# Radix-2 halves for the two transforms over the height

## The chip, the cores and the metric

One core of one Trainium2 chip. The metric is the device time of one launch in microseconds (us). Names of lines (L303) are those of the kernel in question, so the same operation has another line after the change.

## The reference, cut to what matters

Four images of 256 x 256 positions with 64 channels pass through a block with a 2-D FFT and an inverse FFT, then a depthwise convolution, then a second layer. Cut to what the change touches:

```
h  = pw(layernorm(x), w_te)              # x: (4, 256, 256, 64)
F  = fft2(h, axes=(1, 2))                # height and width
fc = gelu(pw(concat(real F, imag F), w_fc))
sp = real(ifft2(re + 1j * im))
x1 = x + pw(sp, w_tp)
d  = gelu(depthwise3x3(pw(layernorm(x1), w_fe)))
out = second_layer(x1 + pw(d, w_fp))     # untouched here
```

The kernel does every transform as matmuls with tables of cosines and sines. The rows of an image lie on 128 partitions in two planes, t = 0 (rows 0 to 127) and t = 1 (rows 128 to 255).

## The kernel before

For each image there is a **forward stage** (layernorm and transform over the height), a **middle stage** (transform over the width, mixing of channels, width transform back) and a **convolution stage** (inverse transform over the height, layernorm, convolution). The forward stage takes 16 columns at a time, which is called a chunk here:

```
def layernorm(pool, src, dst, sq, name):
    nc.vector.tensor_reduce(mean, fl(src), AX.X, ALU.add)              # "mean"
    nc.vector.tensor_scalar(mean, mean, -1.0 / C, None, ALU.mult)      # small op: releases POOL
    nc.gpsimd.tensor_tensor(fl(dst), fl(src), mean..., ALU.add)        # "subtraction"
    nc.scalar.activation(fl(sq), fl(dst), AF.Square)
    nc.vector.tensor_reduce(var, fl(sq), AX.X, ALU.add)                # "variance"
    nc.vector.tensor_scalar(var, var, 1.0 / C, EPS, ALU.mult, ALU.add) # small op: releases POOL
    nc.gpsimd.tensor_tensor(rstd, var, minus_half..., ALU.pow)         # "power"
    nc.vector.tensor_tensor(fl(dst), fl(dst), rstd..., ALU.mult)       # "multiply"
# [...]
for q in range(NCH):                     # 16 chunks; xt has 3 buffers, sq 1, the others 2
    # [...] load xt
    layernorm(pool, rows, rows, sq, n)
    for par, op in enumerate((ALU.add, ALU.subtract)):                 # "first adds"
        nc.vector.tensor_tensor(xb[:, :, par], xt[:, :, 0], xt[:, :, 1], op)
    for par in range(2):
        for m in range(2):
            ps = bank(...)
            for t in range(2):           # the whole height: two matmuls that accumulate
                nc.tensor.matmul(ps, dh[:, t, m * P : (m + 1) * P], xb[:, t, par]...,
                                 start=t == 0, stop=t == 1)
            nc.scalar.copy(yt[:, par, :, m, :], ps...)
    # [...] store yt
```

The order in which each engine gets its instructions is fixed when the kernel is built: the scheduler of the framework interleaves several chunks. The inverse transform, also 16 columns at a time:

```
for w0 in range(0, W, 8):
    for t in range(2):
        ps = bank(...)
        for r, tb in enumerate((ihr, ihi)):      # real and imaginary part, 128 frequencies each
            nc.tensor.matmul(ps, tb[:, t * P : (t + 1) * P], uc[:, w0 : w0 + 8, r, :],
                             start=r == 0, stop=r == 1)
        nc.vector.tensor_tensor(dst, dst, ps, ALU.add)
layernorm(pool, x1, xn, sq, n)
```

## Time and profile before

7713.2 us (median of three, 7713.06 to 7714.08). From the trace, the length of the stages of the second to fourth image, as means. (PE is TensorE, DVE VectorE, ACT ScalarE, POOL GpSimd.) A forward stage is counted from the last matmul of the image before to the first one of the middle stage, a convolution stage from its first matmul to its last:

| stage | us an image | bound by |
|---|---|---|
| forward | 317.6 | a loop of waits between DVE and POOL, 17.3 us a chunk |
| middle (to the first matmul of the next stage) | 579.1 | PE |
| convolution | 827.4 | PE, 50.13 us a period of 16 columns |

In a timeline a row is: start us, length us, engine, line, operation, out<-in, shape, count, and in brackets how long the engine had been idle and what ended that. Two rows whose records overlap by 0.1 us are pipelined. Work per chunk is best read as the difference between starts.

### The profile page before, as it was taken

The numbers are of one execution on the slowest core, as the hardware profiler recorded it, in microseconds if no ns is written. First come the engines' busy times: TensorE is split into PE (matmuls) and PEld (weight loads), VectorE is DVE, ScalarE is ACT, GpSimd is POOL, SyncE is SP. The second block draws the span as 40 slices with busy tenths as digits, with TensorE's granted clock in tenths as the row PEclk, the third lists the DMA queues.
The fourth block names the chain that finished last, engine by engine and source line by source line (L and its number), as shares of the span: only waits on it lengthen the run. The fifth ranks groups of instructions, "written<-read, shape, count | busy, mean of one in ns | idle before, by whom it ended". The sixth has DMA issues, their size and how long they took to land.

```text
span 7717.2 us, 68181 instructions
## 1 busy us (share of the span) xinstructions
PE 6763.2 (88%) x28276; PEld 3952.8 (51%) x28276; DVE 2489.1 (32%) x2808; ACT 1726.7 (22%) x2514; POOL 1864.8 (24%) x718
## 2 busy tenths in 40 slices
PE   4699899994799899984799899975799899988888
PEld 1366555551466455541466455542466455544444
DVE  6433222316433322226333322226333232211111
ACT  2233211112233211112233211112233211111111
POOL 5311222215311222215311222215211222210000
PEclk8899999997899999997899999987899999999999
DMA  3222211223222222123222122213222222225555
GB/s 125 90 55 66 71 55 58 58 45 124 82 66 55 77 61 60 57 48 115 81 60 65 67 66 66 60 39 120 77 56 65 71 61 65 60 62 183 178 182 163
DMA packets 763659, 620.34 MB, mean 80 GB/s; under 512 B 279173, under 2 KB 689239, under 8 KB 754903
## 3 DMA queue, kind: packets, MB, share of 16 engines
q1 hardware_dynamic: 763350, 615.99, 26.5%
q8 instruction: 224, 3.67, 0.2%
q14 instruction: 85, 0.69, 0.0%
HBM read 347.49 MB, written 268.44 MB: 80 GB/s over the span
## 4 chain that ended last, share of the span: by engine, by line
PE 81%; DVE 7%; POOL 5%; issue 3%; DMA 3%; ACT 1%; SPq 0%; POOLq 0%; ACTq 0%; DVEq 0%
PE ps_h L565 17%; PE ps_p L380 12%; PE ps_h L575 9%; PE ps_x L360 6%; PE ps_f L611 6%; PE ps_o L702 6%; PE ps_s_c L509 6%; PE ps_u L443 6%; PE ps_z L426 6%; POOL rstd L273 4%; DVE xt L274 2%; PE ps_h L597 2%; DVE xb L298 2%; PE ps_m L687 2%; PE ps_t L533 2%
## 5 line engine op out<-in xcount | busy, mean ns | idle before, releaser
L565 PE MATMUL ps_h<-tt,wc_main 128*128 128x512 f32 x3072 | 1371.1, 596 | 0.0
L303 PE MATMUL ps_y<-xb,tab 128*128 128x512 f32 x1024 | 565.4, 713 | 642.8 <-DVE xb L298 642.8
L390 ACT ACTIVATE g<-ps_p,b_fc 128x512 f32<-128x512 f32 (+1 forms) x1040 | 709.6, 684 | 1145.0 <-PE ps_p L380 1041.3
L565 PEld LDWEIGHTS ps_h<-tt,wc_main 128*128 128x128 f32 x3072 | 566.2, 189 | 643.4 <-issue 642.5
L575 PE MATMUL ps_h<-tt,wc_half 64*128 64x512 f32 (+1 forms) x3792 | 736.5, 520 | 0.0
L269 POOL TENSOR_TENSOR xn_c<-x_c,mean_c 128x2048 f32<-128x2048 f32 x64 | 231.5, 3617 | 2075.4 <-DVE mean_c L268 1977.1
L303 PEld LDWEIGHTS ps_y<-xb,tab 128*128 128x128 f32 x1024 | 229.4, 232 | 975.9 <-issue 894.5
L396 POOL TENSOR_TENSOR d<-g,g 128x512 f32<-128x512 f32 x260 | 326.7, 1257 | 1665.7 <-ACT g L390 1665.7
L599 ACT ACTIVATE h<-ps_h,b_conv 128x512 f32<-128x512 f32 x512 | 323.0, 681 | 1751.1 <-PE ps_h L597 1751.1
L624 DVE TENSOR_TENSOR st<-x_c,ps_f 128x256 f32<-128x256 f32 x512 | 283.0, 594 | 1291.3 <-PE ps_f L611 1291.3
L575 PEld LDWEIGHTS ps_h<-tt,wc_half 64*128 64x128 f32 x3792 | 414.4, 185 | 349.2 <-issue 319.5
L426 PEld LDWEIGHTS ps_z<-w_tp,d 128*128 128x128 f32 x4064 | 493.7, 192 | 120.3 <-issue 103.3
L380 PE MATMUL ps_p<-xs,wp 128*128 128x512 f32 (+1 forms) x1040 | 528.8, 590 | 0.0
L380 PE MATMUL ps_p<-xs,wm 128*128 128x512 f32 (+1 forms) x1040 | 528.3, 589 | 0.0
L360 PE MATMUL ps_x<-tab,yb 128*128 128x128 f32 x4064 | 510.1, 279 | 0.0
L611 PE MATMUL ps_f<-w_fp,h 128*128 128x64 f32 x4096 | 505.5, 277 | 0.0
L509 PE MATMUL ps_s_c<-uc_c,tab 128*128 128x512 f32 x1024 | 462.7, 606 | 45.3 <-DMA uc_c<-u_d 45.3
L702 PE MATMUL ps_o<-xc,mt 128*128 128x512 f32 x1024 | 456.6, 599 | 50.0 <-DVE mt L695 50.0
L360 PEld LDWEIGHTS ps_x<-tab,yb 128*128 128x128 f32 x4064 | 483.3, 193 | 28.7 <-issue 28.7
L426 PE MATMUL ps_z<-w_tp,d 128*128 128x64 f32 x4064 | 481.7, 272 | 0.9 <-POOL d L396 0.9
L611 PEld LDWEIGHTS ps_f<-w_fp,h 128*128 128x128 f32 x4096 | 477.6, 192 | 0.0
L443 PE MATMUL ps_u<-zt,tab 128*128 128x512 f32 x1024 | 453.5, 596 | 3.5 <-DVE zt L429 3.5
(101 smaller groups left out, 6210.2 us busy)
## 6 DMA issues: line engine op xcount, KB each, us to landing
xt<-in_x_dram SPq DMA_DIRECT2D x128, 512.0 KB, 4.4
y_d<-yt SPq DMA_DIRECT2D x128, 512.0 KB, 2.6
yb<-y_d SPq DMA_DIRECT2D x128, 512.0 KB, 6.6
u_d<-ut SPq DMA_DIRECT2D x128, 512.0 KB, 3.3
uc_c<-u_d SPq DMA_DIRECT2D x64, 1024.0 KB, 4.7
x_c<-in_x_dram SPq DMA_DIRECT2D x64, 1024.0 KB, 7.3
x_d<-st SPq DMA_DIRECT2D x32, 2048.0 KB, 20.8
xc<-x_d SPq DMA_DIRECT2D x128, 512.0 KB, 5.7
```

Of the source, the lines that this page charges most:

```text
L303: nc.tensor.matmul(ps, dh[:, t, m * P : (m + 1) * P], xb[:, t, par].rearrange("p w c -> p (w c)"), start=t == 0, stop=t == 1,)
L360: nc.tensor.matmul(ps[:, j * N + t * P : j * N + (t + 1) * P], blk[:, t, k, lo : lo + 2 * C], tb[:, t, :], start=i == 0, stop=i == 1,)
L380: nc.tensor.matmul(ps[:, :nf], w[:, cols], rhs, start=True, stop=not pr["special"])
L390: nc.scalar.activation(gt[:, :nf], ps[:, :nf], AF.Gelu, bias=b_fc[:, half : half + 1])
L396: eng.tensor_tensor(dt[:, :nf], gl[0][:, :nf], gl[1][:, :nf], op)
L426: nc.tensor.matmul(zv[:, j, 2 * t + r, :], lhs(d, j, t), w_tp, start=True, stop=True)
L443: nc.tensor.matmul(ps, tb[:, t, :], zt[:, t, ri].rearrange("p k c -> p (k c)"), start=ri == 0, stop=ri == 1,)
L509: nc.tensor.matmul(ps, tb[:, t * P : (t + 1) * P], uc[:, w0 : w0 + 8, r, :], start=r == 0, stop=r == 1,)
L565: nc.tensor.matmul(outs[par], wc_main[:, par, dy, :], tt[:, at : at + 2, dy : dy + N], start=dy == 0, stop=False,)
L575: nc.tensor.matmul(outs[par][:, s : s + n, :], wc_half[lo : lo + C, dy, :], tt[lo : lo + C, at : at + n, dy : dy + N], start=False, stop=F ...
L611: nc.tensor.matmul(pv[:, t, 2 * i + par, :], gs[par][:, i, t * P : (t + 1) * P], w_fp, start=True, stop=True,)
L702: nc.tensor.matmul(ps[:, :nf], mt[:, t, to * P : (to + 1) * P], xc[:, t, b0 : b0 + nb2, :].rearrange("p b n -> p (b n)"), start=t == 0, st ...
```

## The change

Radix 2: a transform over 256 rows is split by the parity of the frequency kh. Forward, the sum of the two planes gives the even kh and their difference the odd ones, so two more adds a chunk replace half of the arithmetic, and each matmul makes 64 outputs in its own half of the array's columns. Inverse, the 64 even and 64 odd frequencies are 64 contraction rows each, in their own half of the array's rows; the sum and the difference of the two results give the two planes, made by DVE on evacuation. The intent is to halve PE's time in both.

```
-    dh = np.concatenate([cos[:, :P], -sin[:, :P]], axis=1)
+    kh = np.concatenate([np.arange(0, P, 2), np.arange(1, P, 2)])
+    dh = np.concatenate([cos[:P, kh], -sin[:P, kh]], axis=1)
# [...] the same for the inverse tables
                 for par, op in enumerate((ALU.add, ALU.subtract)):
                     nc.vector.tensor_tensor(xb[:, :, par], xt[:, :, 0], xt[:, :, 1], op)
+                for i, op in enumerate((ALU.add, ALU.subtract)):
+                    nc.vector.tensor_tensor(xh[:, i], xb[:, 0], xb[:, 1], op)   # "new adds"
# [...] forward matmuls
-                        for t in range(2):
-                            nc.tensor.matmul(ps, dh[:, t, m * P : (m + 1) * P], xb[:, t, par]...,
-                                             start=t == 0, stop=t == 1)
+                        for i in range(2):
+                            nc.tensor.matmul(ps[i * C : (i + 1) * C], dh[:, m, i * C : (i + 1) * C],
+                                             xh[:, i, par]..., start=True, stop=True)
# [...] inverse
-                    for t in range(2):
-                        ps = bank(...)
-                        for r, tb in enumerate((ihr, ihi)):
-                            nc.tensor.matmul(ps, tb[:, t * P : (t + 1) * P], uc[:, w0 : w0 + 8, r, :], ...)
-                        nc.vector.tensor_tensor(dst, dst, ps, ALU.add)
+                    pss = [bank(...) for i in range(2)]
+                    for r, tb in enumerate((ihr, ihi)):
+                        for i in range(2):
+                            nc.tensor.matmul(pss[i], tb[i * C : (i + 1) * C],
+                                             uc[i * C : (i + 1) * C, w0 : w0 + 8, r, :], ...)
+                    nc.vector.tensor_tensor(dst, dst, se..., ALU.add)       # even part, both planes
+                    for t, op in enumerate((ALU.add, ALU.subtract)):
+                        nc.vector.tensor_tensor(dst_t, dst_t, so, op)       # odd part
```

More of the change, by code (lines that the diff above doesn't have):

```diff
@@ L41, in _tables @@
     fold = lambda m: m.reshape(2, P, -1).transpose(1, 0, 2).reshape(P, -1)
-    dh = np.concatenate([cos[:, :P], -sin[:, :P]], axis=1)
-    dh[:, P] = cos[:, P]
-    ihr = cos[:P] / NPOS
-    ihi = -sin[:P] / NPOS
+    kh = np.concatenate([np.arange(0, P, 2), np.arange(1, P, 2)])
+    dh = np.concatenate([cos[:P, kh], -sin[:P, kh]], axis=1)
+    dh[:, P] = cos[:P, P]
+    ihr = cos[kh, :P] / NPOS
+    ihi = -sin[kh, :P] / NPOS
     ihr[0] *= 0.5
-    ihi[0] = 0.5 * cos[P] / NPOS
+    ihi[0] = 0.5 * cos[P, :P] / NPOS
     left = KERNEL - 1 - (KERNEL - 1) // 2
@@ L75, in _tables @@
     parts = {
-        "dh": fold(dh),
+        "dh": dh,
         "cw": by_parity(cos),
@@ L287, in conv_seq_kernel @@
                 xb = pool.tile([P, 2, 2, WH, C], F32, tag="xb", name=f"xb_{n}")
+                xh = pool.tile([P, 2, 2, WH, C], F32, tag="xh", name=f"xh_{n}")
                 yt = pool.tile([P, 2, WH, 2, C], F32, tag="yt", name=f"yt_{n}")
@@ L296, in conv_seq_kernel @@
                 layernorm(pool, rows, rows, sq, n)
-                for par, op in enumerate((ALU.add, ALU.subtract)):
-                    nc.vector.tensor_tensor(xb[:, :, par], xt[:, :, 0], xt[:, :, 1], op)
+                for i, op in enumerate((ALU.add, ALU.subtract)):
+                    nc.vector.tensor_tensor(xb[:, :, i], xt[:, :, 0], xt[:, :, 1], op)
+                for i, op in enumerate((ALU.add, ALU.subtract)):
+                    nc.vector.tensor_tensor(xh[:, i], xb[:, 0], xb[:, 1], op)
                 for par in range(2):
@@ L301, in conv_seq_kernel @@
                         ps = bank(f"ps_y_{n}_{par}_{m}")
-                        for t in range(2):
+                        for i in range(2):
                             nc.tensor.matmul(
-                                ps,
-                                dh[:, t, m * P : (m + 1) * P],
-                                xb[:, t, par].rearrange("p w c -> p (w c)"),
-                                start=t == 0,
-                                stop=t == 1,
+                                ps[i * C : (i + 1) * C],
+                                dh[:, m, i * C : (i + 1) * C],
+                                xh[:, i, par].rearrange("p w c -> p (w c)"),
+                                start=True,
+                                stop=True,
                             )
@@ L505, in back_h @@
                 for w0 in range(0, W, 8):
-                    for t in range(2):
-                        ps = bank(f"ps_s_{n}_{w0}_{t}")
-                        for r, tb in enumerate((ihr, ihi)):
+                    pss = [bank(f"ps_s_{n}_{w0}_{i}") for i in range(2)]
+                    for r, tb in enumerate((ihr, ihi)):
+                        for i in range(2):
                             nc.tensor.matmul(
-                                ps,
-                                tb[:, t * P : (t + 1) * P],
-                                uc[:, w0 : w0 + 8, r, :],
+                                pss[i],
+                                tb[i * C : (i + 1) * C],
+                                uc[i * C : (i + 1) * C, w0 : w0 + 8, r, :],
                                 start=r == 0,
@@ L515, in back_h @@
                             )
-                        dst = x1[:, t, w0 : w0 + 8, :].rearrange("p w c -> p (w c)")
-                        nc.vector.tensor_tensor(dst, dst, ps, ALU.add)
+                    se, so = (ps.rearrange("p (w c) -> p w c", c=C) for ps in pss)
+                    dst = x1[:, :, w0 : w0 + 8, :]
+                    nc.vector.tensor_tensor(
+                        dst, dst, se.unsqueeze(1).to_broadcast([P, 2, 8, C]), ALU.add
+                    )
+                    for t, op in enumerate((ALU.add, ALU.subtract)):
+                        dst = x1[:, t, w0 : w0 + 8, :]
+                        nc.vector.tensor_tensor(dst, dst, so, op)
                 layernorm(pool, x1, xn, sq, n)
```

## The prediction

> **What bounds the kernel now.** I read the page's slices first, then the stretches by engine, then the order of instructions on PE and DVE in one stretch of each kind. The slices:
>
> ```profile
> PE   4699899994799899984799899975799899988888
> DVE  6433222316433322226333322226333232211111
> PEclk8899999997899999997899999987899999999999
> ```
>
> Four times, once per image, PE falls to 4 tenths and DVE rises to 6: that is the forward transform over the height (slices 0-1, 9, 18, 27). Between these PE is at 9. The stretches by engine of the first image (forward height; width and mixing; start of the convolution stage; its steady part) say it in us:
>
> ```profile
> 0.00:305.00 305.00, 142.19 (x268) 58.29 (x268) 183.87 (x149) 66.86 (x82) 148.88 (x38) 0.82 0.34 118
> 305.00:880.00 575.00, 566.29 (x2850) 382.03 (x2850) 175.24 (x258) 196.16 (x292) 98.94 (x82) 0.99 0.21 58
> 880.00:1164.00 284.00, 253.37 (x1065) 143.93 (x1064) 81.62 (x92) 46.92 (x67) 82.08 (x25) 0.95 0.25 75
> 1164.00:1720.00 556.00, 555.18 (x2450) 321.98 (x2448) 151.24 (x182) 96.13 (x142) 136.81 (x39) 1.00 0.17 47
> ```
>
> Columns: stretch, length, then busy us of PE, weight load, DVE, ACT, POOL, granted clock, DMA share, GB/s. In the last row PE is busy 555 of 556 us at clock 1.00: **bound by PE**. In the first row PE is busy under half and no engine is full: **a chain of waits**.
>
> The change touches one group of matmuls in each kind: L303 (forward) and L509 (inverse, in the PE-bound part). In order of time on PE, one period of 16 columns of the convolution stage begins:
>
> ```profile
> 1161.93 1.92 PE L533 MATMUL ps_t<-ident,xn_c 128*128 128x128 f32 x16
> 1163.68 7.03 PE L509 MATMUL ps_s_c<-uc_c,tab 128*128 128x512 f32 x16
> 1170.55 5.31 PE L565 MATMUL ps_h<-tt,wc_main 128*128 128x512 f32 x12
> ...
> 1196.64 2.85 PE L575 MATMUL ps_h<-tt,wc_half 64*128 64x512 f32 x12
> 1199.41 0.61 PE L597 MATMUL ps_h<-tab,r_edge 128*128 128x4 f32 x4
> ```
>
> The next L509 starts at 1213.81, a period of 50.13 us. Read the starts: sixteen full matmuls of L509 take 1170.55-1163.68 = 6.87 us; twelve *half* matmuls of L575 (64 contraction rows, the two halves of the array in turn, into two banks) take 1199.41-1196.64 = 2.77 us, so 0.231 us each against 0.429 for a full one. The kernel already shows the concurrency that the change counts on. (A float32 matmul shows as two instructions.)
>
> In the forward stage, DVE in order of time:
>
> ```profile
> 1898.47 2.29 DVE L274 TENSOR_TENSOR xt<-xt,rstd 128x2048 f32<-128x2048 f32 x1 [5.68 <-POOL rstd L273]
> 1900.67 2.28 DVE L271 TENSOR_REDUCE var<-sq 128x32 f32<-128x2048 f32 x1
> 1902.87 2.35 DVE L298 TENSOR_TENSOR xb<-xt 128x1024 f32<-128x1024 f32 x2
> 1905.14 0.17 DVE L272 TENSOR_SCALAR var<-var 128x32 f32<-128x32 f32 x1
> 1905.22 0.17 DVE L268 TENSOR_SCALAR mean<-mean 128x32 f32<-128x32 f32 x1
> 1910.90 5.70 DVE L274 TENSOR_TENSOR xt<-xt,rstd 128x2048 f32<-128x2048 f32 x1 [5.51 <-POOL rstd L273]
> ```
>
> DVE works, releases POOL's 5.4 us power (L273), waits for it, works again: a loop DVE, POOL, DVE. The pattern repeats every five chunks (the 5.79 us pairs of L298 start at 1879.09 and 1965.54): 86.45 us, 17.3 us a chunk of 16 columns. DVE's waits in these five are 1.02+5.68+5.51+5.47+8.98+3.40 = 30.1 us, 6.0 a chunk. The other images have the same period.
>
> **What the Trainium skill says.**
> 1. TensorEngine Tiling (Array Packing), Overview and Key Properties: a dimension of at most 64 allows up to 2x, tiles run in parallel, and changing the mode drains the array. The trace agrees with the 2x (0.231 against 0.429 to 0.442 us) and shows no drain worth counting: the 2.77 us of L575 includes the way into it and out. It shows column halves only once, in the weight preparation (four 128*64 matmuls of 256 columns in 1.12 us, 658 ns each alone).
> 2. The same page, PSUM Bottleneck: tiling does not speed up evacuation. That is this change's cost on DVE.
> 3. VectorE: DVE Perf Modes, the TRN2 errata: a float32 tensor_tensor takes (N+151)/0.96 ns. For N=1024 that is 1.22 us; the trace has 1.218 (L298). For 2048, 2.29 us; the trace has 2.29 where nothing disturbs it.
> 4. SBUF — State Buffer, Who interferes with whom: a DVE instruction with two SBUF inputs contends with a GpSimd one that reads SBUF. The trace agrees: the L274 above lasts 5.70 us while POOL runs the 3.62 us L269 from 1910.84, and 2.29 when POOL runs the power.
>
> **The change part by part.**
>
> *Inverse height (L509).* As many instructions (1024), each over 64 rows, alternating halves and banks as L575 does. A period's sixteen become 16 x 0.231 = 3.70 us instead of 6.87: **3.17 us off PE's path** per steady period. Per image there are 16: the first is not steady (PE starts cold, 8.94 us, then waits 19.5 us for the layernorm), the second is cold too (8.13 us from start to next start, so about 4 saved), 14 are steady: 14 x 3.17 = 44.4. For the first, what counts is when DVE has the sum: now at 901.44, 9.7 us after the matmuls' start; afterwards two rounds of 1.22+0.69+0.69 = 2.6 us, the first beginning after about 2.3 us: 7.5 us, so 2 saved. Together 50 us an image, **200 us** in all.
>
> *Its evacuation.* DVE had four ops of 512 a period (0.69 us, 2.75). It gets, twice, one of 1024 (estimate from row 3 above: 1.22) and two of 512: 5.2 us, 2.4 more per 47 us, beside 13.6 that it is busy there now (151/556 x 50). It hides: the layernorm is done at 1190.15 and needed by L533 at 1212.05, 22 us of slack; the sum itself ends no later than now, because its matmuls end sooner. Banks: eight in rotation, and evacuation of the convolution's next ones is unchanged. **0 us.**
>
> *Forward height, PE (L303).* As many instructions, half the columns of the array each. PE is not the bound. Only the last chunk of an image is exposed: 292.05 to 302.16, 10.1 us cold, then y_d is stored and read back. Halved: 5 saved, less the 2.35 of the new adds: about 2.5 an image, **10 us** in all.
>
> *Forward height, DVE.* Two more tensor_tensor of 1024 a chunk, 2.35 us as the pair of L298: 64 x 2.35 = 150 us of DVE work, in the stage that waits on DVE and POOL. If it always lies between the old adds and the small op that releases POOL, the loop grows by all of it: +150. If it always lies in the wait for POOL, it costs 0: there are 6.0 us of waits a chunk. In the five-chunk pattern the adds come directly before the small releasing ops twice (as at 1905.14) and before a further reduction three times. The new adds need both old ones, so an instruction that is ready may go between: where that is the releasing op, they fall into the wait (two of five hidden), where it is a reduction they stand before the release (three of five exposed). That is 0.6 x 150 = 90; a fuller DVE should also have its reductions ready earlier and move some more of the releases ahead. I take half: **+75 us**. This is a choice, not a reading.
>
> Sum: -200 + 0 - 10 + 75 = -135; 7713 - 135 = **7578**, put at 7580.
>
> **The rivals.**
> *The forward adds are exposed in full, or worse.* For: every L298 in the pattern is followed within 5 us by a release of POOL. Worse if they run beside L269 on POOL, as one pair of five does now (5.79 instead of 2.35): 3.4 us each. Then +150 to +190, and 7660 to 7690. Against: 6 us of idle DVE per chunk.
> *They hide.* DVE's waits have room for all of them; then 7713-200-10 = 7505.
> *The halves do not run side by side in L509*, because of a drain or because the moving operand is strided over two planes. Then the 200 us vanish and the kernel is 50 to 150 us slower. Against: L575 shows the concurrency beside the same neighbours, and L509 now reads the same strided operand at full rate.
> *DVE becomes the bound of the convolution stage.* Against: 27% busy there, 22 us of slack. I give it little.
> *The throttle takes the gain.* L575's dense halves run at clock 1.00; little.
>
> **Range and chances.** Nearly all the spread is the forward adds: 0 to +150 gives 7505 to 7655; the inverse's 200 may be off by 15. I take 7525 to 7650. Faster by over 2% means below 7559, so the forward adds may cost at most about 55 us: 0.36. Slower by over 2% needs rival three: 0.01. The rest, 0.63, is within 2%.
>
> **What would show it.** L509 in order of time: 16 in 3.7 us, a steady period of about 47 us with PE still full. L517 split into 1024- and 512-wide ops, with L533 waiting no more than now. In the forward stage: a five-chunk period between 86 and 98 us, of which I expect 92; DVE busier by 2.35 us a chunk, and its waits for rstd shorter where the adds hid. After the last adds, PE's tail about 5 us. The prediction is wrong if the period of the convolution stage does not fall by 3 us, or if the order of DVE in the forward stage changes so far that the five-chunk pattern leaves that range.

## The result

The changed kernel takes 7688.7 us (median of four, 7687.3 to 7690.2), the kernel before 7713.1 on the same chip. The ratio is 0.9969 (95% interval 0.9951 to 0.9986). Ratios here are the mean time of one kernel's fast runs over that of the other's of the same rounds, so not quite the ratio of the medians. The time lies above the range that was predicted. All outputs are right.

The two busy rows of the page by slices:

```profile
PE   2499899982599899982599899973599899988888
DVE  6533333327533333327533333327533333311111
```

PE falls deeper than before in the forward stages (2 and 5 tenths where it had 4 and 7), and DVE is at 7 and 5 there where it was at 6 and 3. The stretches by engine, for the first forward stage and for the steady part of the convolution (columns as in the prediction):

```profile
0.00:351.00 351.00, 108.65 (x268) 46.05 (x268) 236.12 (x182) 66.87 (x82) 145.04 (x39) 0.72 0.31 108
1190.00:1700.00 510.00, 510.00 (x2377) 297.97 (x2376) 167.01 (x195) 94.18 (x138) 136.33 (x39) 1.00 0.17 50
```

The first stage is 351 us long and not 313, with a quarter less PE busy time in it (109 us; 142 before). The convolution stage is still bound by PE in full, at full clock. PE in order of time in that stage:

```profile
1230.18 1.92 PE L547 MATMUL ps_t<-ident,xn_c 128*128 128x128 f32 x16
1232.03 3.70 PE L517 MATMUL ps_s_c<-uc_c,tab 64*128 64x512 f32 x16
1235.66 0.70 PE L579 MATMUL ps_h<-tt,wc_main 128*128 128x512 f32 x1
```

Sixteen half matmuls take 1235.66 - 1232.03 = 3.63 us where the full ones took 6.87, and a period takes 47.09 us. DVE in the forward stage, one chunk from multiply to multiply:

```profile
1905.33 5.70 DVE L277 TENSOR_TENSOR xt<-xt,rstd 128x2048 f32<-128x2048 f32 x1 [5.52 <-POOL rstd L276]
1910.95 2.27 DVE L270 TENSOR_REDUCE mean<-xt 128x32 f32<-128x2048 f32 x1
1913.14 2.34 DVE L302 TENSOR_TENSOR xb<-xt 128x1024 f32<-128x1024 f32 x2
1915.41 2.27 DVE L274 TENSOR_REDUCE var<-sq 128x32 f32<-128x2048 f32 x1
1917.61 2.34 DVE L304 TENSOR_TENSOR xh<-xb 128x1024 f32<-128x1024 f32 x2
1919.87 0.17 DVE L275 TENSOR_SCALAR var<-var 128x32 f32<-128x32 f32 x1
1919.96 0.17 DVE L271 TENSOR_SCALAR mean<-mean 128x32 f32<-128x32 f32 x1
1925.64 5.70 DVE L277 TENSOR_TENSOR xt<-xt,rstd 128x2048 f32<-128x2048 f32 x1 [5.52 <-POOL rstd L276]
```

And POOL over the same time:

```profile
1920.18 5.42 POOL L276 TENSOR_TENSOR rstd<-var,minus_half 128x32 f32<-128x32 f32 x1 [11.31 <-DVE mean L271]
1925.58 3.62 POOL L272 TENSOR_TENSOR xt<-xt,mean 128x2048 f32<-128x2048 f32 x1
```

The pattern of five chunks is gone. In the steady part, all but the first few chunks and the last of an image, every chunk now looks like this and takes 1925.64 - 1905.33 = 20.31 us. Two things are to be seen. The new adds (L304) stand *between* the variance (L274) and the small op (L275) for which POOL's power waits, so POOL starts 2.27 us later than it could; in the whole program this is so in 55 of 63 places. And in the steady part the power and the subtraction follow each other on POOL, so the subtraction runs into the multiply (in 51 of 64 chunks), which takes 5.70 us instead of 2.29.

Per chunk, in us, with DVE's waits and collisions read from the brackets and lengths and the rest as its own work:

| | before (five chunks / 5) | after |
|---|---|---|
| waits of DVE | 30.06 / 5 = 6.01 | 5.52 |
| collisions with the subtraction (before: two multiplies and one pair of first adds in five chunks) | (2 x 3.41 + 3.43) / 5 = 2.05 | 3.41 |
| own work | 9.23 | 11.39 |
| sum | 17.29 | 20.32 |

The wait has hardly become shorter. The new adds lie on top of it. By stage, us an image (means of images two to four), the whole comes to:

| | before | after | difference, all four images |
|---|---|---|---|
| forward | 317.6 | 358.3 | +160.5 |
| middle | 579.1 | 578.9 | -0.9 |
| convolution | 827.4 | 779.8 | -190.2 |

With 1.4 us more after the last image this is -29.2; the two profiled spans differ by 29.3 (7717.2 and 7687.9). The medians differ by 24.4: the profiled launch of the kernel before took 7719.0 us, 6 more than the median.

### The profile page after: what moved, and what is told of

It is laid out like the page before. It is cut to its first block, busy times and chain, and to the rows that moved or that the text cites. A ratio compares the mean times of both kernels' runs of the same rounds, so it can differ in the third digit from the quotient of the medians.

```text
span 7687.9 us, 68585 instructions
## 1 busy us (share of the span) xinstructions
PE 6413.8 (83%) x28276; PEld 3797.7 (49%) x28276; DVE 2823.9 (37%) x3064; ACT 1729.7 (22%) x2514; POOL 1850.1 (24%) x718
## 4 chain that ended last, share of the span: by engine, by line
PE 78%; DVE 8%; POOL 5%; issue 5%; DMA 3%; ACT 1%; SPq 0%; POOLq 0%; ACTq 0%; DVEq 0%
PE ps_h L579 17%; PE ps_p L387 12%; PE ps_h L589 9%; PE ps_x L367 6%; PE ps_f L625 6%; PE ps_o L716 6%; PE ps_u L450 6%; PE ps_z L433 6%; POOL rstd L276 4%; PE ps_s_c L517 3%; DVE xb L302 2%; PE ps_h L611 2%; DVE xh L304 2%; PE ps_m L701 2%; DVE mean L270 2%
## 5 line engine op out<-in xcount | busy, mean ns | idle before, releaser
L310 PE MATMUL ps_y<-xh,tab 128*64 128x512 f32 x1024 | 415.1, 877 | 956.7 <-DVE xh L304 912.1
L310 PEld LDWEIGHTS ps_y<-xh,tab 128*64 128x64 f32 x1024 | 173.7, 199 | 1195.1 <-issue 1144.9
L276 POOL TENSOR_TENSOR rstd<-var,minus_half 128x32 f32<-128x32 f32 x64 | 350.1, 5470 | 622.4 <-DVE mean L271 533.0
```

The source lines that it names most:

```text
L276: nc.gpsimd.tensor_tensor(rstd, var, minus_half.to_broadcast([P, 2 * W]), ALU.pow)
L310: nc.tensor.matmul(ps[i * C : (i + 1) * C], dh[:, m, i * C : (i + 1) * C], xh[:, i, par].rearrange("p w c -> p (w c)"), start=True, stop=True,
```

## The experiments

Two theories were set against each other. **Order**: the adds cost what they do because of where the built order puts them, before the release of POOL. **Work**: they cost what they last, since DVE and POOL alternate in a loop whatever the order. The runs were made each beside the kernel before, which took 7717.2 to 7717.9 us there. Forward and convolution are us an image from the traces, as in the table above.

| kernel | us | ratio to before | forward | us a chunk | convolution |
|---|---|---|---|---|---|
| before | 7713.1 | 1 | 317.6 | 17.29 | 827.4 |
| after | 7688.7 | 0.9969 | 358.3 | 20.32 | 779.8 |
| inv_only | 7527.8 | 0.9754 | 317.0 | | 779.8 |
| fwd_only | 7880.9 | 1.0212 | 358.9 | 20.32 | 827.2 |
| adds_only | 7882.4 | 1.0214 | 359.2 | 20.32 | 827.2 |
| adds_twice | 7630.3 | 0.9887 | 342.4 | 18.1 | 780.2 |
| hand_same | 7724.9 | 1.0009 | 365.4 | 20.32 | 779.5 |
| hand_moved | 7654.4 | 0.9918 | 348.1 | 19.11 | 779.5 |
| late | 7563.9 | 0.9800 | 327.4 | 16.9 | 779.8 |
| inv_blocked | 7529.8 | 0.9756 | 317.0 | | 781.1 |
| hand_apart | 7563.4 | 0.9801 | 324.8 | 17.15 | 780.2 |
| deep | 7234.3 | 0.9375 | 242.0 | 12.90 | 779.7 |
| deep_halves | 7384.9 | 0.9569 | 279.9 | 15.29 | 779.6 |
| deep2 | 7178.4 | 0.9301 | 227.6 | 11.11 | 779.9 |

### Each part alone: inv_only and fwd_only

inv_only is the changed kernel with the forward loop of before; its table keeps the new order of kh:

```
-                        for i in range(2):      # halves, from xh
+                        for t in range(2):      # whole, from xb; no xh, no new adds
```

> The inverse transform in halves, the forward one whole as before (its table only has the kh in the new order). If the two parts act in separate stages, the convolution stage keeps the 47.5 us an image that the changed kernel's trace shows and the forward stage returns to about 317 us an image: 7713 - 4 x 47.5 = 7523 us. Rival: the shorter convolution stage moves something in the next image's forward stage; then the forward stage is not at 317 us and the time is off 7523 by more than 10 us.

Measured 7527.8 against 7717.6, so 189.9 us less; the forward stage is back at 317.0. fwd_only is the counterpart, with the inverse loop of before:

> The forward transform in halves with its new adds, the inverse one whole as before. If the parts are additive: forward stage as in the changed kernel, 358 us an image instead of 317, convolution period 50.13 us: 7713 + 160 = 7873 us. Rival as for inv_only: off by more than 10 us.

Measured 7880.9, 163.3 us more. The two add up to -26.6, and the whole change made -24.4: **the parts are additive**, and the forward one takes back what the inverse one gives.

### The adds alone: adds_only

The kernel before, with the new adds made and their result left unused; all matmuls whole:

```
+                for i, op in enumerate((ALU.add, ALU.subtract)):
+                    nc.vector.tensor_tensor(xh[:, i], xb[:, 0], xb[:, 1], op)
```

> The kernel before with the two new adds of a chunk made and not used; its matmuls stay whole. Theory 'the adds alone' (in the order in which they were queued on DVE): the order on DVE is that of the changed kernel, so a chunk takes 20.3 us and the last adds come 45 us later per image; without the shorter matmul tail of the changed kernel that is 7713 + 4 x 45 = 7893 us. Rival 'the half matmuls cost it' (column halves, switching, later PE start): then the adds alone cost little and the time is within 30 us of 7713.

Measured 7882.4, the same as fwd_only within 1.5 us, and the same 20.32 us a chunk. So the half matmuls neither cost nor gain anything to speak of in the forward stage, and the whole loss is the adds. The expected 7893 took 45 us an image, and the stage grew by 41 to 42.

### The adds made twice: adds_twice

The changed kernel with the loop of the new adds written out a second time. This tells the theories apart, since they expect opposite signs.

> The changed kernel with the two new adds of a chunk made twice, the same values into the same place: 2.3 us more DVE work a chunk. Theory 'work' (the adds cost what they last, as they stand in a loop of DVE and POOL): a chunk takes 20.3 + 2.3 = 22.6 us, 7689 + 64 x 2.3 = 7835 us. Theory 'order' (what counts is which instruction stands between the end of one chunk's work and the small ops that release POOL for the next): the compiled order of DVE is another one here, in groups of three chunks; laying the durations of the traces out in that order I estimate 18.0 us a chunk and a forward stage about 20 us an image shorter than the changed kernel's: 7689 - 79 = 7610 us, faster with twice the adds.

Measured 7630.3: **58 us faster than the changed kernel with twice its adds**. Work as an account of the loss has fallen. DVE in order of time:

```profile
1857.71 2.35 DVE L302 TENSOR_TENSOR xb<-xt 128x1024 f32<-128x1024 f32 x2
1859.97 0.17 DVE L275 TENSOR_SCALAR var<-var 128x32 f32<-128x32 f32 x1
1860.06 0.17 DVE L271 TENSOR_SCALAR mean<-mean 128x32 f32<-128x32 f32 x1
1860.15 2.40 DVE L304 TENSOR_TENSOR xh<-xb 128x1024 f32<-128x1024 f32 x2
1862.48 2.35 DVE L306 TENSOR_TENSOR xh<-xb 128x1024 f32<-128x1024 f32 x2
1866.70 5.70 DVE L277 TENSOR_TENSOR xt<-xt,rstd 128x2048 f32<-128x2048 f32 x1 [1.87 <-POOL rstd L276]
```

Here the small ops come first, and 4.6 us of adds lie in the wait for the power, of which 1.87 us are left. The scheduler chose this order in 33 of 63 places, and the one that delays the power in 19. The estimate was 20 us too low; it had left out that the power takes 6.38 us here (in 16 chunks of 64), which the next pair takes up.

### One thing moved: hand_same and hand_moved

To be sure that it is the place and not something else in the new order, the forward loop was written with its order on DVE and POOL fixed by hand. hand_same fixes the steady order of the changed kernel. hand_moved differs from it in one place:

```
                 var(q + 1)
-                fold_h(q)            # the new adds
-                matmuls(q)
                 vsc(q + 1)           # small op: releases the power
                 msc(q + 2)           # small op: releases the subtraction
                 power(q + 1)
                 sub(q + 2)
+                fold_h(q)
+                matmuls(q)
```

> The changed kernel with the order on DVE and POOL in the forward stage fixed by hand, and fixed to the one that the compiled kernel had in its steady part (multiply, next but one mean, first adds, next variance, new adds, then the two small ops that release POOL). A control: a chunk takes 20.3 us as in the changed kernel. The changed kernel had its first three chunks in a quicker order (last adds of the first three 31 us after the start where this one needs about 67 for three), so the stage is about 15 us an image longer: 7689 + 60 = 7749 us. If fixing the order costs something of its own, a chunk is over 20.6 us.

> As hand_same, with one thing moved: the two new adds stand behind the two small ops that release POOL, not before them. Same instructions, same work. Theory 'order': the 2.27 us of the adds fall into the wait for POOL's power, a chunk takes 20.32 - 2.27 = 18.05 us, the stage is about 34 us an image shorter than hand_same's: 7749 - 136 = 7613 us. Theory 'work' (DVE and POOL have this much to do whatever the order): no change, 7749 us. That 18.05 is still over the 17.3 of the kernel before would be the multiply that collides with POOL's subtraction in every chunk.

hand_same measured 7724.9: 20.32 us a chunk, so fixing the order costs nothing of its own in the steady part. The stage is 7 us longer than the changed kernel's in images two to four, not 15; in the first image it is 15. hand_moved measured 7654.4, **70 us less with the same instructions**. That is the theory of order, but only half of the expected 136. DVE and POOL of hand_moved show why:

```profile
1856.20 0.18 DVE L339 TENSOR_SCALAR var<-var 128x32 f32<-128x32 f32 x1
1856.30 0.17 DVE L324 TENSOR_SCALAR mean<-mean 128x32 f32<-128x32 f32 x1
1856.38 2.40 DVE L365 TENSOR_TENSOR xh<-xb 128x1024 f32<-128x1024 f32 x2
1862.92 5.70 DVE L351 TENSOR_TENSOR xt<-xt,rstd 128x2048 f32<-128x2048 f32 x1 [4.14 <-POOL rstd L343]
```

```profile
1856.53 6.36 POOL L343 TENSOR_TENSOR rstd<-var,minus_half 128x32 f32<-128x32 f32 x1 [9.17 <-DVE mean L324]
1862.86 3.61 POOL L329 TENSOR_TENSOR xt<-xt,mean 128x2048 f32<-128x2048 f32 x1
```

The power takes 6.36 us here instead of 5.42. Of the 2.27 us that are hidden, 0.94 come back this way; a chunk gains 20.32 - 19.11 = 1.21 (the last 0.1 is not accounted for).

What lengthens it is the one add that is already running when the power starts, 0.15 us after the adds do, and not adds beside it as such. adds_twice has powers of both kinds. Above, its adds start at 1860.15 and the power at 1860.29: 6.38 us. In the next chunk they start two microseconds into the power, which then takes 5.42:

```profile
1877.09 5.42 POOL L276 TENSOR_TENSOR rstd<-var,minus_half 128x32 f32<-128x32 f32 x1 [6.84 <-DVE var L275]
1879.07 2.34 DVE L304 TENSOR_TENSOR xh<-xb 128x1024 f32<-128x1024 f32 x2
1881.33 2.35 DVE L306 TENSOR_TENSOR xh<-xb 128x1024 f32<-128x1024 f32 x2
```

Of the 896 powers of the forward stages in the fourteen traces, 267 start while an add or a multiply of DVE is running. All of these are lengthened (5.98 to 7.56 us), each by what is left of that one instruction less 0.14 us. In 137 an add or a multiply starts only after the power did: 5.41 to 5.43 us, as in the 492 with neither beside them. The "Who interferes with whom" section of the Trainium skill's "SBUF — State Buffer" says that a DVE instruction with two SBUF inputs contends with a GpSimd one that reads SBUF; the traces agree, and who starts first decides who waits. So the place that would hide the adds in full is just behind the start of the power. No run was made to test that for hand_moved. The trace of before had one such power in each image, in the timeline of POOL, behind the start of a pair of first adds at 1767.87, and it was not read:

```profile
1767.95 6.41 POOL L273 TENSOR_TENSOR rstd<-var,minus_half 128x32 f32<-128x32 f32 x1 [2.50 <-DVE mean L268]
```

### The collision with the subtraction: hand_apart

hand_moved with the small op on the mean behind the multiply, so that POOL's subtraction is not ready when the power ends:

```
             mult(q)
+            msc(q + 1)
+            sub(q + 1)
             mean(q + 2)
             fold_w(q)                # the first adds
             var(q + 1)
             vsc(q + 1)
-            msc(q + 2)
             power(q + 1)
-            sub(q + 2)
             fold_h(q)
```

> As hand_moved, with one more thing moved: the small op on the mean, which releases POOL's subtraction, stands behind the multiply instead of before it. POOL then has no subtraction ready when its power ends, and the multiply should take 2.29 us in place of 5.70; the subtraction meets the first adds instead and holds them for about 1.4 us. hand_moved measured 19.10 us a chunk; if the collision costs what the trace shows, 19.10 - 3.41 + 1.4 = 17.1 us, about 31 us an image less: 7654 - 125 = 7530 us. If the collision only takes the place of a wait, nothing is won: 7654 us.

17.15 us a chunk, as expected. DVE:

```profile
1848.10 2.29 DVE L351 TENSOR_TENSOR xt<-xt,rstd 128x2048 f32<-128x2048 f32 x1 [4.14 <-POOL rstd L343]
1852.59 3.80 DVE L358 TENSOR_TENSOR xb<-xt 128x1024 f32<-128x1024 f32 x2
```

The multiply is at 2.29 us, and the first adds take 3.80 instead of 2.34. So the collision is a cost of its own, which the changed kernel pays in full in every chunk. The time, 7563.4, is 91 us less than hand_moved's where 125 were expected. The stage is shorter by 23.3 us an image. The expectation counted 2.0 us in all sixteen chunks, 31 us; only some fourteen are steady, which would be 27, and the start and end of an image give the other 4 back.

### Left to the scheduler, from other source: late

The new adds and matmuls of a chunk written after the layernorm and first adds of the next one, with no order fixed:

```
+                if waiting is not None:
+                    forward_h(*waiting)      # new adds and matmuls of the chunk before
+                waiting = q, xb
```

> The changed kernel with the new adds and the matmuls of a chunk written in the source after the layernorm and first adds of the next chunk; the order is left to the compiler. It makes groups of three chunks in which the new adds mostly stand in waits; laying the durations of the traces out in that order I estimate 16.5 us a chunk, 38 us an image less than the changed kernel: 7689 - 153 = 7536 us. Theory 'work': 7689 us or more.

Measured 7563.9, 125 us less than the changed kernel for moving a few lines of source. The expectation was 28 us too low, by 0.4 us a chunk (16.9, not 16.5); this estimate too had the power at 5.42, and 23 of the 64 take 6.26 to 6.41.

### How the halves must be queued: inv_blocked

inv_only with both matmuls of the one half queued before both of the other:

```
-                    for r, tb in enumerate((ihr, ihi)):
-                        for i in range(2):
+                    for i in range(2):
+                        for r, tb in enumerate((ihr, ihi)):
```

> The kernel with the halves in the inverse transform alone (inv_only, 7528 us), its matmuls in another order: both of the upper half of the rows, then both of the lower half, in place of turn about. If the halves run side by side only when they alternate, the sixteen of a period take up to 6.9 us again and the time goes up by up to 64 x 3.24 = 207 us, to 7735. If the array reaches far enough ahead, nothing changes: 7528 us.

Measured 7529.8 against inv_only's 7527.8. A period is 47.19 us instead of 47.09, and the sixteen take 3.74 us instead of 3.63. At this distance the two halves of the array run side by side whether or not they alternate. How far the distance may grow, no run shows.

### Without waits: deep, deep_halves and deep2

If waits are what the order makes, an order with more chunks in flight should do without them, and the adds should then cost their full length. deep is inv_only with the forward stage ordered by hand, five input buffers and two for the squares:

```
for q in range(-3, NCH):
    var(q + 1); vsc(q + 1); power(q + 1)
    mean(q + 3); msc(q + 3); sub(q + 3)
    mult(q); fold_w(q); matmuls(q)
```

> The halves in the inverse transform alone (inv_only, 7528 us), and the forward stage, whole as before, in an order by hand with three more chunks in flight (variance of q+1, mean of q+3, then multiply and first adds of q; five input buffers, two of squares). Theory 'order': the stage is then bound by the work of DVE and POOL, 9.1 us and 9.0 to 10 us a chunk (the longer where DVE's adds delay the power as hand_moved showed, 6.36 us), so about 10 us a chunk in place of 17.3: about 100 us an image less, 7528 - 400 = 7130 us. Rivals: the transfers (1 MB in and 1 MB out a chunk, some 200 GB/s) or PE on its slow clock (about 9 us a chunk) bound it before that, at 11 to 13 us a chunk: 7200 to 7300 us.

Measured 7234.3, with 12.90 us a chunk. It is faster than anything before it, and slower than expected. The numbers lie where the rivals put them, but the reason is one that neither names:

```profile
1718.32 2.28 DVE L351 TENSOR_TENSOR xt<-xt,rstd 128x2048 f32<-128x2048 f32 x1
1720.70 5.78 DVE L358 TENSOR_TENSOR xb<-xt 128x1024 f32<-128x1024 f32 x2
```

In the steady part DVE never waits any more, for POOL, PE or a transfer, but the first adds meet the subtraction every time (5.78 instead of 2.35). Now the forward halves with their new adds are put into this order, directly behind the first adds:

> deep with the forward transform in halves too: the new adds directly behind the first adds, matmuls of half width as in the changed kernel. In deep DVE does not wait in the steady part (12.90 us a chunk, all of it its own instructions, 3.43 of it one collision with POOL's subtraction). So here, unlike in the order of the changed kernel, no wait is left that could hide the adds, and they should cost what they last: 12.90 + 2.27 = 15.17 us a chunk, 7234 + 64 x 2.27 = 7379 us, less about 8 for the shorter matmul tail: 7371 us. If the adds cost little even here, the account of waits is wrong.

Measured 7384.9 (expected 7371), 15.29 us a chunk (expected 15.17). **Where DVE has no waits, the new adds cost their length: 2.39 us a chunk, 150 us in all.** The same adds cost 3.03 us a chunk in the changed kernel and 1.21 less than that after one move in its order. So work does bound a good order; it did not bound the order that was built.

deep2 takes deep and moves the subtraction beside the reductions:

```
for q in range(-4, NCH):
    var(q + 1); vsc(q + 1); power(q + 1)
    mult(q); fold_w(q)
    msc(q + 3); sub(q + 3)
    mean(q + 4)
    matmuls(q)
```

> deep (inverse in halves, forward whole) with POOL's subtraction released behind the first adds and the next mean taken there, so that it runs beside DVE's two reductions, which in the traces it does not hold up. The collision of 3.43 us goes; the power now runs beside the multiply and the adds and takes about 6.36 us as in hand_moved. POOL then has 3.62 + 6.36 = 9.98 us a chunk and is the bound: about 10.0 us in place of 12.90, 13 steady chunks x 2.9 = 38 us an image, 7234 - 151 = 7083 us. Rival: PE on its slow clock (9.6 us a chunk in deep) or the transfers bound it first: 11 us or more a chunk, over 7120 us.

Measured 7178.4, the best kernel here: 7.0% less than before. It misses the expected 7083 by 95 us, and POOL says why:

```profile
1701.99 7.33 POOL L343 TENSOR_TENSOR rstd<-var,minus_half 128x32 f32<-128x32 f32 x1 [0.18 <-DVE var L339]
1709.30 3.61 POOL L329 TENSOR_TENSOR xt<-xt,mean 128x2048 f32<-128x2048 f32 x1
```

The first adds are free of the subtraction, but the power takes 7.33 us, not 6.36. DVE shows where that comes from:

```profile
1711.02 1.93 DVE L339 TENSOR_SCALAR var<-var 128x32 f32<-128x32 f32 x1
1712.87 2.28 DVE L351 TENSOR_TENSOR xt<-xt,rstd 128x2048 f32<-128x2048 f32 x1
```

The small op now falls into the subtraction (1709.30 to 1712.91) and takes 1.93 us instead of 0.18: it ends when the subtraction does. The multiply follows it at 1712.87 and so is running when the next power starts, at 1713.10; this power waits out the rest of the multiply and takes 7.34 us. It is the rule of hand_moved again, with a longer instruction in the way. POOL is busy but for 0.18 us, as expected, but with 3.61 + 7.33 + 0.18 = 11.12 us a chunk, of which 1.9 are this wait. The rival's number came out (11 us or more), not its reason: DVE waits for no transfer in the steady part, and PE waits for the first adds.

## Why the prediction was wrong

**The inverse transform: right in mechanism, 10 us too large.** A steady period gives 50.13 - 47.09 = 3.04 us and not 3.17. L517 alone saves 3.24 (6.87 to 3.63), but its neighbours take longer: the transposes ahead of it 1.85 us instead of 1.75, the matmuls after it 5.35 instead of 5.24. That I take to be what entering and leaving the half-row mode costs, 0.2 us a period; no run isolates it. The prediction called the drain not worth counting from 2.77 us for L575. That is a time from start to start of the half matmuls alone, and the 0.2 us do not show in it, as they do not show in L517's 3.63: they lie in the neighbours. The first period of an image gives 0.6 us instead of 2, the second 4.3 as against 4. In all 47.5 us an image, 190 instead of 200; inv_only measured 189.9.

**Its evacuation: right.** PE is full in the steady part (510.00 of 510.00 us), so the extra DVE work is hidden there.

**The shorter tail of the forward matmuls: wrong by most of its 10 us.** From the end of the last first adds to the first matmul of the next stage the second image took 18.2 us before and 18.2 after; all four together save 2.5 us. In the second image the sixteen matmuls at the end went from 8.8 to 6.8 us, not to half, and the new adds took up the rest. The halves do run side by side: a pair of halves takes 0.85 us on a granted clock of 0.5 (1.00 is full speed), as one whole matmul does. But the granted clock was 0.81 over the sixteen whole ones, half of which ran at full clock (0.43 us each), and 0.61 over the halves. adds_only and fwd_only, whole and half matmuls with the same adds, are within 1.5 us of each other.

**The forward adds: the step that failed.** The prediction put down "I take half: +75 us. This is a choice, not a reading." The four forward stages grew by 160.5 us (adds_only: 165.4), which is twice that, and with it the time left the range. Three parts of that step were wrong:

1. It kept the five-chunk pattern of before and placed the adds into it. But the order is built anew for the changed program. What came out has one chunk as its period (five take 101.6 us, outside the 86 to 98 that the prediction had named as its test), and in 55 of 63 places the adds are before the release. Of the two hidden in five that were counted on, almost none is left. The rival "exposed in full, or worse" was the one that happened, with 3.03 us a chunk against the 2.35 of the adds themselves, and its 7660 to 7690 us hold the result. The worse part has another cause than the rival gave, though: not the new adds meet the subtraction, but the multiply does.
2. It had read the collision of multiply and subtraction, but did not cost it: two in five chunks before (and one of the first adds), it became one in each, +1.36 us a chunk (the table above). hand_apart shows that it is a cost of its own.
3. It took adds in the wait as free. They are only if they start after the power: started just before it, 0.94 us of the 2.27 come back in a longer power (hand_moved).

It also reasoned that a fuller DVE would move releases ahead. adds_twice did just that, with twice the adds; the changed kernel did not. **Why the scheduler chose the one order for the one and another for the other is not shown by any run here**; what is shown is that the order decides.

Two slips in the working changed little. The multiply is said to take 2.29 us "when POOL runs the power"; in the trace of before no multiply ran beside a power (all 42 at 2.29 us ran with POOL idle), though later traces bear it out (96 that started within a power took 2.28 to 2.32 us). And +150 to +190 for the adds give 7653 to 7693 us, not 7660 to 7690.

The rivals of a serialised inverse, of DVE as the bound of the convolution and of a slower clock did not occur in the inverse: 3.63 us, PE full, clock 1.00.

## What to carry to other kernels

Before an instruction is added to an engine in a loop of waits, ask which small op on that engine releases the other one, and on which side of it the new instruction will stand. The sum of the work does not tell, the pattern of the old trace does not carry over, and a scheduler may answer differently to every change; where it matters, fix the order. Halve the matmuls where PE is the bound, and leave them whole where it is not: the inverse half alone is some 160 us better than both. And count as busy not only an instruction's own time, but what it does to one on an engine that shares its port: here 0.15 us in the start of an add or a multiply decided whether the power took 5.42 us or up to 7.56.

## What the Trainium skill lacked or had wrong

- "SBUF — State Buffer", SBUF: two separate sides: it says that whichever of two contending instructions starts first has the shared ports for the whole instruction, and the other blocks. The traces agree where the subtraction is first (the multiply takes 5.70 us for 2.29) and where DVE is first (267 powers waited out the rest of the DVE instruction, less 0.14 us). They differ where a power over 32 elements is first: 96 multiplies that started within the 5.42 us of one took 2.28 to 2.32 us, as alone. Why, no run shows.
- "TensorEngine Tiling (Array Packing)", Key Properties: it says that a change of mode drains the array, without a cost. Here the matmuls ahead of the halves and behind them took about 0.1 us longer each, which may be that cost; no run isolates it.
- "TensorEngine Tiling (Array Packing)", Overview: up to 2x for a dimension of 64, and no page has a measured figure for two tiles. For rows the matmuls here went from 6.87 to 3.63 us (1.9x); for columns a pair of halves took 0.85 us, as one whole matmul did at the same granted clock of 0.5 (2x).
- Beyond who takes the shared ports first, no page here treats the order that a scheduler builds as a cost of its own: the same instructions took 7724.9 or 7654.4 us, depending on the place of one pair of adds.
